# Layer 0 attention: the value product of a query tile once for all eight key/value heads, on four column groups, with the transposed probabilities in one tile per key tile

## The chip, the core and the metric

The kernel runs on one core of a Trainium2 chip. The core has five engines with an instruction stream each: TensorE (PE in the profile, with its weight loads as PEld), VectorE (DVE), ScalarE (ACT), GpSimd (POOL) and SyncE (SP), which issues most of the DMAs. Each works through its own stream in order and waits for the others through semaphores. The metric is the device time of one execution in microseconds (us), lower is better. A time of a kernel is the median of several executions; a profile is one further execution with the hardware profiler on.

## The reference, cut to what matters

Two transformer layers on 4 sequences of 256 tokens with 512 features, all in float32. Each layer is an attention and a feed-forward product, each followed by a residual sum and a layer norm without scale. The change is in the attention of layer 0, which has 32 query heads of 16 features that share 8 key/value heads in groups of 4, with a causal mask:

```python
q = (x @ Wq + bq).reshape(B, S, NUM_HEADS, HEAD_DIM).transpose(0, 2, 1, 3)
k = (x @ Wk + bk).reshape(B, S, NUM_KV_HEADS, HEAD_DIM).transpose(0, 2, 1, 3)
v = (x @ Wv + bv).reshape(B, S, NUM_KV_HEADS, HEAD_DIM).transpose(0, 2, 1, 3)
...
scores = jnp.where(causal, scores, NEG)
p = jax.nn.softmax(scores, axis=-1)
out = jnp.einsum('bhqk,bhkd->bhqd', p, v)
out = out.transpose(0, 2, 1, 3).reshape(B, S, D_MODEL)
return out @ Wo + bo
```

Layer 0 goes on with a feed-forward product whose weight is dequantised in the kernel. Layer 1 has an attention with 32 heads of 128 features and a product with a ternary weight.

## The kernel before, in words

The function `block_kernel` writes both layers as one program. The order of each engine's instructions is fixed when the program is built, by a planner that follows the order of the code and moves instructions where it expects them to be ready earlier.

**Steps of layer 0.** The attention of layer 0 is cut into 64 steps `(b, qt, h, i)`: sequence `b` (0 to 3; called a column here, a sequence's two query tiles of 128 tokens), query tile `qt` (0 or 1), half `h` of the key/value heads (heads 0 to 3 or 4 to 7), and `i`, the place of the query head in its group of four. A step so has four query heads, one for each key/value head of its half. With the causal mask query tile 0 needs key tile 0 alone, query tile 1 needs key tiles 0 and 1; a step of tile 1 is twice as wide.

**What a step does.** `begin0` (L473): two matmuls make the scores of four heads (L482, on two row groups of 32 rows), DVE adds the mask (L487) and takes the negative row maxima (L490), ACT takes four exponentials with their sums (L274). Dividing by the sums (`divided`, L278: a reciprocal on DVE at L279, a product on POOL at L282) is put off to the next step. `transpose0` (L506): TensorE transposes the four heads' probabilities, one key tile to a PSUM bank (L297), and DVE and ACT in turn copy the banks to SBUF (`evacuate`, L95; its instructions show as L100 on DVE and L102 on ACT). `end0` (L520): at the last `i` of a half, the values are multiplied with the transposed probabilities of the four places `i` together (L531).

**The value product.** A key/value head has 16 features, and two of them (even and odd, `e` = 0 and 1) share 32 output partitions: the weights `v` of one head are 128 keys x 32, with zeros in the 16 columns of the other head. Each matmul has 128 rows, 32 columns and 512 moving elements (4 places x 128 queries) and writes 32 of the 128 partitions of one PSUM bank `o`: partitions `32 * r` on, where `r = 2 * h + j` is a pair of heads. So a half `h` writes two of the four groups of 32 columns, in turn, and the other half writes the other two, four steps later. After the second half the bank is copied to `oT` and a `tail0` generator is started.

**The pipeline.** `run` (L323) does, for each n: begin step n, one piece of fill work, transpose step n - 3 (`lag=3`), end step n - 5 (`lag` and `more=2`). Fill work is the projections of the next column (`project0`: L386, L399, L414) and the tails (`tail0`: output product L438, residual sum L440, norm L257 to L264, transpose L270, feed-forward product L455, sum L459, second norm, transpose to `x2T`).

**Buffers.** The scores have two PSUM tiles of two banks each (`ps_s0`), so the scores of step n wait for the exponentials of step n - 2. Three banks (`ps_w`) go round among transposes and products. One bank is for `o` (`ps_o0`). The transposed probabilities of a half are one SBUF tile with room for two key tiles, `[P, 2, G, 4, 4, 32]`, 16 KB a partition, in two buffers.

**After layer 0.** Layer 1 begins with its projections in Strassen's form (`Quarters`, L619, products L632) beside the last tails, and then runs 64 steps of its own attention (L968 to L1027) with the output product in Strassen's form (L881).

Of the kernel before, what the change touches and what calls it, by code (L numbers as in the profile page):

```python
# [12 lines left out]
F32 = mybir.dt.float32  # L13
# [7 lines left out]
P = 128  # L21
# [3 lines left out]
NKV, G = 8, 4  # L25
BLK = 32
ROWS = 64
EPS = 1e-5
MASKED = -3.0e38

# [19 lines left out]
def distance_table():  # L52

    rel = P + np.arange(P)[:, None] - np.arange(2 * P)[None, :]
    dist = -np.sqrt(np.maximum(rel, 0).astype(np.float32))
    return np.where(rel >= 0, dist, np.float32(MASKED)).astype(np.float32)


@with_exitstack
def block_kernel(  # L60
# [23 lines left out]
    def pool(stack, name, bufs=1, **kw):  # L84
        return stack.enter_context(tc.tile_pool(name=name, bufs=bufs, **kw))
# [9 lines left out]
    def evacuate(dst, src):  # L95

        if not last:
            turn[0] ^= 1
        if turn[0] and not last:
            nc.vector.tensor_copy(dst, src)  # L100
        else:
            nc.scalar.copy(dst, src)  # L102
# [20 lines left out]
    a0 = pool(la, "a0", 2, side="right")  # L123
    causal = wa.tile([P, P], F32, name="causal")
    make_causal_mask(nc, causal, MASKED)
    ps_w = pool(ctx, "ps_w", 3, space=PSUM)
    ps_s0 = pool(la, "ps_s0", 2, space=PSUM)
    ps_o0 = pool(la, "ps_o0", 1, space=PSUM)
# [5 lines left out]
    def bank_m(name):  # L134
        return ps_w.tile([P, D], F32, tag="w", name=name)
# [116 lines left out]
    def norm_factors(y, name):  # L252

        st = s0.tile([P, 6], F32, tag="bn", name=f"bn_{name}", bufs=4)
        mv = s0.tile([P, 2], F32, tag="mv", name=f"mv_{name}", bufs=4)
        rs = s0.tile([P, 1], F32, tag="rs", name=f"rs_{name}", bufs=4)
        nc.vector.bn_stats(st, y)  # L257
        nc.vector.bn_aggr(mv, st)
        nc.vector.tensor_scalar(rs, mv[:, 1:2], EPS, 1.0, ALU.add, ALU.mult)
        powers.append(nc.gpsimd.tensor_tensor(rs, rs, minus_half, ALU.pow))  # L260
        return mv[:, 0:1], rs

    def normalise(dst, y, factors):
        nc.vector.tensor_scalar(dst, y, *factors, ALU.subtract, ALU.mult)  # L264

    def transposed(dst, src, name):

        pt = bank_t(f"pt_{name}")
        for c in range(NC):
            nc.tensor.transpose(pt[:, c, :], src[:, ts(c, P)], ident)  # L270
        evacuate(dst, pt)
# [20 lines left out]
    def transposed_probabilities(name, pr, parts):  # L292

        for kt, dst in parts:
            pt = bank_t(f"pt_{name}_{kt}")
            for i in range(G):
                nc.tensor.transpose(pt[:, i, :], pr[:, i, ts(kt, P)], ident)  # L297
            evacuate(dst, pt.rearrange("p i (j q) -> p i j q", q=32))
# [135 lines left out]
    def tail0(tt, oT):  # L434

        py = bank_m(f"py_{tt}")
        for i in range(G):
            nc.tensor.matmul(py, oT[:, i, :], wop[:, i, :], start=(i == 0), stop=(i == G - 1))  # L438
        y = s0.tile([P, D], F32, tag="y", name=f"y_{tt}")
        nc.vector.tensor_tensor(y, py, x[tt], ALU.add)  # L440
        factors = norm_factors(y, f"a{tt}")
        yield True
        x1 = s0.tile([P, D], F32, tag="x1", name=f"x1_{tt}")
        normalise(x1, y, factors)
        yield True
        if tt < NTT - 1:
            yield True
            yield True
        x1T = s0.tile([P, NC, P], F32, tag="x1T", name=f"x1T_{tt}")
        transposed(x1T, x1, f"x1_{tt}")  # L450
        nc.gpsimd.tensor_tensor(x1, x1, fb_b, ALU.add)
        yield True
        pf = bank_m(f"pf_{tt}")
        for c in range(NC):
            nc.tensor.matmul(  # L455
                pf, x1T[:, c, :], wfT[:, c, :], start=(c == 0), stop=(c == NC - 1)
            )
        y2 = s0.tile([P, D], F32, tag="y", name=f"y2_{tt}")
        nc.vector.tensor_tensor(y2, pf, x1, ALU.add)  # L459
        factors = norm_factors(y2, f"b{tt}")  # L460
        yield True
        x2[tt] = xp.tile([P, D], F32, tag="x", name=f"x2_{tt}")
        normalise(x2[tt], y2, factors)
        yield True
        if tt < NTT - 1:
            yield True
            yield True
        transposed(x2T[:, :, ts(tt, P)], x2[tt], f"x2_{tt}")
        yield True

    ahead, tails = deque(), deque()
# [25 lines left out]
    open0 = {}  # L497
# [8 lines left out]
    def transpose0(b, qt, h, i, pr):  # L506
        name = f"0_{b}_{qt}_{h}_{i}"
        if i == 0:
            open0["p", h] = a0.tile(
                [P, 2, G, 4, 4, 32], F32, tag="prT", name=f"prT0_{b}_{qt}_{h}"  # L510
            )
        prT = open0["p", h]
        transposed_probabilities(
            name,
            pr,
            [(kt, prT[:, kt, i].rearrange("p j n q -> p n j q")) for kt in range(qt + 1)],
        )
        return prT

    def end0(b, qt, h, i, prT):  # L520
        if i < G - 1:
            return
        if h == 0:
            open0["o"] = ps_o0.tile([P, G * P], F32, tag="o", name=f"o0_{b}_{qt}")
        o = open0["o"]
        v = qkv0[b][2]
        for kt in range(qt + 1):
            for e in range(2):
                for j in range(2):
                    r = 2 * h + j  # L530
                    nc.tensor.matmul(  # L531
                        o[32 * r : 32 * r + 32, :],
                        v[:, kt, r, ts(e, 32)],
                        prT[:, kt, :, :, 2 * j + e, :],
                        start=(kt == 0 and e == 0),
                        stop=(kt == qt and e == 1),
                    )
        if h == 1:
            oT = a0.tile([P, G, P], F32, tag="oT", name=f"oT0_{b}_{qt}")
            evacuate(oT.rearrange("p i q -> p (i q)"), o)  # L540
            tails.append(tail0(2 * b + qt, oT))

    def before0(step):
        b, qt, h, i = step
# [11 lines left out]
    def fill():  # L556
# [6 lines left out]
        [(b, qt, h, i) for b in range(B) for qt in range(2) for h in range(2) for i in range(G)],  # L563
        begin0,
        transpose0,
        end0,
        before0,
        fill,
# [534 lines left out]
```

## Time and profile before

| | |
|---|---|
| median of 3 executions | 973.0 us (971.88 to 973.82) |
| profiled execution, own time | 970.91 us |
| its span | 968.9 us |
| PE busy | 939.5 us, 97% |
| DVE busy | 619.7 us, 64% |
| POOL busy | 445.6 us, 46% |
| ACT busy | 316.3 us, 33% |
| DMA, mean | 77 GB/s |
| granted TensorE clock, mean | 0.995 |

The span runs from the first to the last recorded instruction; the device time has some 2 us more around it. A float32 matmul shows as two records (two passes), each with a weight load of its own. Matmul durations are modelled and reach past the start of the next matmul, so a busy share of PE includes short stalls. The attention of layer 0 ends at about 276 us of the span.

### The profile page before, as it was taken

The numbers are of one execution on the slowest core, as the hardware profiler recorded it, in microseconds if no ns is written. First come the engines' busy times: TensorE is split into PE (matmuls) and PEld (weight loads), VectorE is DVE, ScalarE is ACT, GpSimd is POOL, SyncE is SP. The second block draws the span as 40 slices with busy tenths as digits, with TensorE's granted clock in tenths as the row PEclk, the third lists the DMA queues.
The fourth block names the chain that finished last, engine by engine and source line by source line (L and its number), as shares of the span: only waits on it lengthen the run. The fifth ranks groups of instructions, "written<-read, shape, count | busy, mean of one in ns | idle before, by whom it ended". The sixth has DMA issues, their size and how long they took to land.

```text
span 968.9 us, 11389 instructions
## 1 busy us (share of the span) xinstructions
PE 939.5 (97%) x3593; PEld 556.0 (57%) x3593; DVE 619.7 (64%) x1291; ACT 316.3 (33%) x1194; POOL 445.6 (46%) x461
## 2 busy tenths in 40 slices
PE   7999999999899999999999999999999999999996
PEld 5645555554344445566666666666666666666652
DVE  3876767777633446665666665766676666666566
ACT  2664564555511002333222222122222212224441
POOL 3463552644446213444533553444633634556732
PEclk9999999999999999999999999999999999999998
DMA  9500000000020011354443443433443334332001
GB/s 237 185 1 1 1 1 1 1 1 1 1 87 0 22 44 39 103 139 120 122 134 90 123 133 109 130 109 87 131 130 91 128 77 119 113 105 69 1 33 55
DMA packets 76418, 74.45 MB, mean 77 GB/s; under 512 B 5957, under 2 KB 52678, under 8 KB 76358
## 3 DMA queue, kind: packets, MB, share of 16 engines
q1 hardware_dynamic: 75014, 72.02, 26.1%
q10 hardware_dynamic: 1344, 1.70, 0.6%
q8 instruction: 29, 0.48, 0.2%
q14 instruction: 31, 0.25, 0.1%
HBM read 49.58 MB, written 24.12 MB: 76 GB/s over the span
## 4 chain that ended last, share of the span: by engine, by line
PE 82%; POOL 9%; DVE 5%; ACT 2%; DMA 1%; issue 1%; ACTq 0%; POOLq 0%; DVEq 0%
PE p_q L632 18%; PE po L881 14%; PE sc L968 7%; PE o L1008 7%; PE p_k L632 5%; PE p_v L632 5%; PE o L531 5%; PE sc L482 4%; PE pt L297 3%; PE pq L399 3%; PE py L438 3%; PE pf L455 3%; PE py L842 2%; POOL pr L282 2%; POOL x L903 2%; ACT pr L274 1%
## 5 line engine op out<-in xcount | busy, mean ns | idle before, releaser
L274 ACT ACTIVATE pr<-sc,nm 128x256 f32<-128x256 f32 (+1 forms) x512 | 209.4, 420 | 364.7 <-DVE nm L984 277.2
L282 POOL TENSOR_TENSOR pr<-pr,sums 128x512 f32<-128x512 f32 (+1 forms) x128 | 190.1, 1485 | 232.1 <-DVE sums L279 223.9
L976 DVE SCALAR_TENSOR_TENSOR sc<-table,sc 128x128 f32<-128x128 f32 (+1 forms) x256 | 86.0, 356 | 34.7 <-PE sc L968 32.4
L274 ACT ACTIVATION_READ_ACCUMULATOR pr<-sc,nm 128x1 f32 x512 | 103.5, 202 | 0.0
L968 PEld LDWEIGHTS sc<-kT,qT 128*128 128x128 f32 x512 | 82.3, 191 | 35.1 <-issue 29.7
L968 PE MATMUL sc<-kT,qT 128*128 128x256 f32 (+1 forms) x512 | 95.0, 327 | 0.0
L1008 PE MATMUL o<-prT,v 128*128 128x512 f32 x192 | 92.8, 592 | 0.0
L308 DVE STREAM_TRANSPOSE blocks<-pr 128x512 f32<-128x512 f32 x84 | 57.6, 698 | 45.2 <-POOL pr L282 45.2
L646 DVE TENSOR_TENSOR qT<-p_q,qT 128x512 f32<-128x512 f32 x96 | 64.6, 685 | 33.6 <-PE p_q L632 32.8
L984 DVE TENSOR_REDUCE nm<-sc 128x2 f32<-128x512 f32 (+1 forms) x128 | 69.9, 550 | 1.5
L297 PE MATMUL pt<-ident,pr 128*128 128x128 f32 x432 | 62.6, 278 | 6.0 <-POOL pr L282 5.3
L297 PEld LDWEIGHTS pt<-ident,pr 128*128 128x128 f32 x432 | 49.3, 142 | 32.5 <-issue 17.1
L490 DVE TENSOR_REDUCE nm<-sc 128x4 f32<-128x512 f32 (+1 forms) x64 | 61.0, 953 | 1.1
L482 PE MATMUL sc<-kT,qT 32*128 32x256 f32 (+1 forms) x256 | 59.9, 533 | 1.6 <-ACT pr L274 1.6
L487 DVE TENSOR_TENSOR sc<-sc,causal 128x512 f32<-128x512 f32 x64 | 44.3, 692 | 26.5 <-PE sc L482 26.2
L881 PE MATMUL po<-wo,so 128*128 128x256 f32 x224 | 58.0, 381 | 2.1 <-POOL so L612 2.1
L632 PE MATMUL p_q<-x2T,ws_q 128*128 128x512 f32 x128 | 59.8, 592 | 0.0
L102 ACT COPY o<-o 128x512 f32<-128x512 f32 x29 | 17.0, 586 | 124.9 <-PE o L1008 124.9
L632 PE MATMUL p_q<-xt,ws_q 128*128 128x512 f32 x128 | 57.7, 592 | 0.0
L881 PE MATMUL po<-wo,o 128*128 128x256 f32 x224 | 57.7, 380 | 0.0
L632 PE MATMUL p_q<-x2T,wq 128*128 128x512 f32 x128 | 57.6, 592 | 0.0
L881 PE MATMUL po<-to,so 128*128 128x256 f32 x224 | 53.3, 381 | 1.0 <-POOL so L615 1.0
(155 smaller groups left out, 1435.2 us busy)
## 6 DMA issues: line engine op xcount, KB each, us to landing
way<-blocks SPq DMA_DIRECT2D x112, 128.0 KB, 2.5
prT<-way SPq DMA_DIRECT2D x28, 512.0 KB, 3.7
wq<-in_L_attn_w_qkv_dram SPq DMA_DIRECT2D x8, 1024.0 KB, 5.3
wo<-in_L_attn_w_o_dram SPq DMA_DIRECT2D x8, 1024.0 KB, 5.4
way<-blocks SPq DMA_DIRECT2D x112, 64.0 KB, 1.8
prT<-way SPq DMA_DIRECT2D x28, 256.0 KB, 2.6
wk<-in_L_attn_w_qkv_dram SPq DMA_DIRECT2D x4, 512.0 KB, 3.7
wv<-in_L_attn_w_qkv_dram SPq DMA_DIRECT2D x2, 1024.0 KB, 6.3
```

Of the source, the lines that this page charges most:

```text
L274: nc.scalar.activation(pr[:, i, 0:w], sc, AF.Exp, bias=nm[:, i : i + 1], accum_out=sums[:, i : i + 1])
L282: nc.gpsimd.tensor_tensor(pr[:, :, 0:w], pr[:, :, 0:w], sums.unsqueeze(2).to_broadcast([P, G, w]), ALU.mult)
L297: nc.tensor.transpose(pt[:, i, :], pr[:, i, ts(kt, P)], ident)
L482: nc.tensor.matmul(sc[:, j, :, 0:w], qT[rows, i, ts(qt, P)], kT[rows, :, 0:w], start=True, stop=True)
L490: nc.vector.tensor_reduce(nm, scf[:, :, 0:w], AX.X, ALU.max, negate=True)
L632: nc.tensor.matmul(bank, fixed, moving, start=(c == 0), stop=(c == 1))
L646: add = lambda dst, a, b: nc.vector.tensor_tensor(dst, a, b, ALU.add)
L881: nc.tensor.matmul(bank[:, ts(n, HALF)], left[:, c, :], right[:, c, :], start=(c == 0), stop=(c == 1),)
L968: nc.tensor.matmul(sc[:, m, 0:w], qT[:, 2 * j + m, b * S + qt * P : b * S + (qt + 1) * P], kT[:, b * S : b * S + w], start=True, stop=True,)
L976: nc.vector.scalar_tensor_tensor(sc[:, m, 0:w], table[:, 2 * P - w :], slopes[kv * G + 2 * j + m], sc[:, m, 0:w], ALU.mult, ALU.add,)
L984: nc.vector.tensor_reduce(nm[:, 2 * j : 2 * j + 2], sc[:, :, 0:w], AX.X, ALU.max, negate=True)
L1008: nc.tensor.matmul(o, v1[:, 2 * b + kt, ts(kv, P)], prT[:, kt].rearrange("p j h q -> p h j q"), start=(kt == 0), stop=(kt == qt),)
```

## The change

`end0` now returns at once except at the last step of a query tile, `(h, i) == (1, 3)`. There it does the value product of all eight key/value heads: for each key tile (now from the last to the first) and each parity, four matmuls in the order `r = 2, 3, 0, 1`, one on each group of 32 columns. The matmuls themselves, their shapes, number and the bank they write are as before. `transpose0` writes to tiles of one key tile, `[P, G, 4, 4, 32]`, 8 KB a partition, one for each half and key tile, from five buffers, and hands on the tiles of both halves.

```diff
         if i == 0:
-            open0["p", h] = a0.tile(
-                [P, 2, G, 4, 4, 32], F32, tag="prT", name=f"prT0_{b}_{qt}_{h}"
-            )
-        prT = open0["p", h]
+            open0[h] = [
+                a0.tile(
+                    [P, G, 4, 4, 32], F32, tag="prT", name=f"prT0_{b}_{qt}_{h}_{kt}", bufs=5
+                )
+                for kt in range(qt + 1)
+            ]
         transposed_probabilities(
             name,
             pr,
-            [(kt, prT[:, kt, i].rearrange("p j n q -> p n j q")) for kt in range(qt + 1)],
+            [(kt, open0[h][kt][:, i].rearrange("p j n q -> p n j q")) for kt in range(qt + 1)],
         )
-        return prT
+        return open0[0], open0[1] if h else None
 
     def end0(b, qt, h, i, prT):
-        if i < G - 1:
+        if (h, i) != (1, G - 1):
             return
-        if h == 0:
-            open0["o"] = ps_o0.tile([P, G * P], F32, tag="o", name=f"o0_{b}_{qt}")
-        o = open0["o"]
+        o = ps_o0.tile([P, G * P], F32, tag="o", name=f"o0_{b}_{qt}")
         v = qkv0[b][2]
-        for kt in range(qt + 1):
+        for kt in range(qt, -1, -1):
             for e in range(2):
-                for j in range(2):
-                    r = 2 * h + j
+                for r in (2, 3, 0, 1):
                     nc.tensor.matmul(
                         o[32 * r : 32 * r + 32, :],
                         v[:, kt, r, ts(e, 32)],
-                        prT[:, kt, :, :, 2 * j + e, :],
-                        start=(kt == 0 and e == 0),
-                        stop=(kt == qt and e == 1),
+                        prT[r // 2][kt][:, :, :, 2 * (r % 2) + e, :],
+                        start=(kt == qt and e == 0),
+                        stop=(kt == 0 and e == 1),
                     )
-        if h == 1:
-            oT = a0.tile([P, G, P], F32, tag="oT", name=f"oT0_{b}_{qt}")
-            evacuate(oT.rearrange("p i q -> p (i q)"), o)
-            tails.append(tail0(2 * b + qt, oT))
+        oT = a0.tile([P, G, P], F32, tag="oT", name=f"oT0_{b}_{qt}")
+        evacuate(oT.rearrange("p i q -> p (i q)"), o)
+        tails.append(tail0(2 * b + qt, oT))
```

## The prediction

> **What bounds the kernel now.** I read the page first: shares of the engines, then the chain of work that ended last.
>
> ```profile
> PE 939.5 (97%) x3593; PEld 556.0 (57%) x3593; DVE 619.7 (64%) x1291; ACT 316.3 (33%) x1194; POOL 445.6 (46%) x461
> PE 82%; POOL 9%; DVE 5%; ACT 2%; DMA 1%; issue 1%; ACTq 0%; POOLq 0%; DVEq 0%
> PE p_q L632 18%; PE po L881 14%; PE sc L968 7%; PE o L1008 7%; PE p_k L632 5%; PE p_v L632 5%; PE o L531 5%; PE sc L482 4%; PE pt L297 3%; PE pq L399 3%; PE py L438 3%; PE pf L455 3%; PE py L842 2%; POOL pr L282 2%; POOL x L903 2%; ACT pr L274 1%
> ```
>
> TensorE is the bound, and the value product of layer 0 (o, L531) has 5% of the span on the chain, 48 us. Groups of the first 330 us (busy us, mean ns of one record | idle before) and busy times by stretch (PE, PEld, DVE, ACT, POOL) show how nearly all of it is on the path:
>
> ```profile
> L531 PE MATMUL o<-prT,v 128*32 128x512 f32 x192 | 47.7, 607 | 0.6 <-DVE prT L100 0.6
> L438 PE MATMUL py<-wop,oT 128*128 128x512 f32 x64 | 29.6, 605 | 1.3 <-DVE oT L100 1.3
> ...
> 40.00:280.00 240.00, 232.48 (x1104) 119.14 (x1101) 167.77 (x316) 128.76 (x506) 112.38 (x86) 0.99 0.00 1
> ```
>
> 192 records are 96 matmuls of two passes. In layer 0 PE has 97%, DVE 70%, ACT 54%, POOL 47%: there is room, but the other engines are not far behind. The timeline of one burst (start, us) says how fast the passes go:
>
> ```profile
> 52.37 1.91 PE L531 MATMUL o<-prT,v 128*32 128x512 f32 x8
> 54.21 1.13 PE L482 MATMUL sc<-kT,qT 32*128 32x512 f32 x4
> ...
> 52.37 0.14 PEld L531 LDWEIGHTS o<-prT,v 128*32 128x32 f32 x4 [0.17 <-issue]
> 52.82 0.12 PEld L531 LDWEIGHTS o<-prT,v 128*32 128x32 f32 x2 [0.31 <-issue]
> 53.25 0.12 PEld L531 LDWEIGHTS o<-prT,v 128*32 128x32 f32 x2 [0.31 <-issue]
> ```
>
> Eight passes take 1.84 us to the next work; eight passes of py, the same length over all 128 columns, show as 3.70. Two weight loads, 0.11 each, fit in 0.12, and a new pair comes every 0.43. So the two column groups of a half run side by side, a pair of passes each 0.43 us, and the other two groups stand idle. Sequence by sequence the chain has two bursts of 1.84 (tile 0) and two of 3.56 (tile 1).
>
> **The Trainium skill.** "TensorE: Matmul & The Clock Gate", Part 3 (Packing small matmuls): matmuls on different column groups run concurrently, measured 2.38x with three groups and 10.6x with sixteen row-and-column tiles. The pairs above agree for two; no run here shows four. "TensorEngine Tiling (Array Packing)", Key Properties: tiles load weights and multiply independently, changing the tiling mode drains the array. The trace agrees in kind: each burst begins with a gap before its loads, 0.17 above. The first page, Part 1: after an idle window the clock falls to half. The trace shows it once, 0.96 granted in 240 to 280 us. It matters at the end.
>
> **The change, part by part.** *Removed:* the bursts of the first half, one for each query tile. 96 of the 192 passes, 48 pairs of 0.43 us = 20.6 us, with their beginnings 4 x (1.84 + 3.56) = 21.6. *Added:* the same passes join the second half's bursts. If four groups run as two do, a round of four takes 0.43 and those bursts keep 1.84 and 3.56; a stagger of some 7 ns a group is nothing. Copies into the new tiles have the same number and size. Five buffers are enough: four tiles of a tile-1 group and the first of the next group, or two and the first two of the next, never more than five, so no wait is added. Last key tile first means that the first matmul waits for the newest copy, but transposes run two steps ahead of ends, over 3 us: free; without that cover, a copy (0.6 to 0.7) at each of eight bursts, 5 us. No DMA moves and no queue but the engines' own changes.
>
> So the ceiling is 21.6, and the question is what waits next at each removed burst. The next scores need the exponentials of two steps before, so each site has its own slack.
>
> *First column, tile 0 (39.6 us).* Later scores start 2.9, 1.6, 1.5 and 0.2 us after their banks were free, and those banks move up too. I give 0.2 back: **1.65** of 1.84.
>
> *Tile 1, three times (68, 134, 201 us, alike).* PE, then ACT:
>
> ```profile
> 134.58 3.63 PE L531 MATMUL o<-prT,v 128*32 128x512 f32 x16
> 138.14 0.70 PE L482 MATMUL sc<-kT,qT 32*128 32x256 f32 x4
> 138.77 0.66 PE L270 MATMUL pt_x<-ident,x 128*128 128x128 f32 x4
> 139.26 1.04 PE L297 MATMUL pt<-ident,pr 128*128 128x128 f32 x8
> 140.23 0.70 PE L482 MATMUL sc<-kT,qT 32*128 32x256 f32 x4
> 140.86 3.70 PE L455 MATMUL pf<-wfT,x1T 128*128 128x512 f32 x8
> ...
> 135.59 0.21 ACT L274 ACTIVATION_READ_ACCUMULATOR pr<-sc,nm 128x1 f32 x1
> 137.61 0.21 ACT L274 ACTIVATION_READ_ACCUMULATOR pr<-sc,nm 128x1 f32 x1
> ```
>
> The scores at 138.14 need exponentials that end at 135.80, those at 140.23 need 137.82. In the changed order pt_x moves ahead of the first, one matmul of pf ahead of the second, and ACT copies x1T before the second's exponentials (0.6 later, 138.4). From 134.58: pt_x to 135.1; wait, scores 135.85 to 136.5; transposes to 137.35; one pf matmul to 138.2; scores 138.45 to 139.1; three pf matmuls of 0.86 to 141.7. Before, pf ended at 140.86 + 3.43 = 144.3. **2.5** each of 3.56 (worked 2.6).
>
> *Tile 0 of columns 1 and 2 (101, 168 us).*
>
> ```profile
> 101.47 1.91 PE L531 MATMUL o<-prT,v 128*32 128x512 f32 x8
> 103.31 1.13 PE L482 MATMUL sc<-kT,qT 32*128 32x512 f32 x4
> ...
> 105.39 1.13 PE L482 MATMUL sc<-kT,qT 32*128 32x512 f32 x4
> ...
> 104.77 0.21 ACT L274 ACTIVATION_READ_ACCUMULATOR pr<-sc,nm 128x1 f32 x1
> ```
>
> The scores at 105.39 need exponentials that end at 104.98, of scores older than the burst: they can't move. Again one pf matmul (0.86) goes ahead of them and fills the gap; pf ends at 108.8 for 109.9. **1.1** of 1.84.
>
> *Their second bursts.* ACT now does a step's exponentials before the copy of `oT`, and half of a later score pair stands ahead of py: py 1.1 later. But DVE then takes mask and row maxima before the norm's last operation, whose wait for POOL (0.67) and the work around it come off the chain: 1.4 earlier. **0.3** each, the least certain term.
>
> *Last column.* No projections are left. DVE runs nearly full between its two tails, and a walk through it leaves 0.7 at the py of 246.5. Behind, PE waits for POOL at 258.3, the half clock comes, and o of the first half holds PE from 261.3 to 265.6; pf starts at 266.95. Without it, pf starts at about 261.4, when its input is copied, and the last o at 267.2 for 272.07: **4.9** in all, with the clock's fall kept.
>
> Sum: 1.65 + 3 x 2.5 + 2 x 1.1 + 2 x 0.3 + 4.9 = 16.85; I take 16.5. What follows is PE work of layer 1 in an unchanged order; its value weights load when layer 0's memory comes free (issued 280.3, used at 294.6) and so move with it. Span 968.9 - 16.5 = 952.4, own time 970.9 - 16.5 = 954.4. The median of the runs is 2.1 above the profiled execution: 973.0 - 16.5 = **956.5 us**.
>
> **Rivals.** *Nothing is given back:* the ceiling, 951.4. For it: all bursts of the first half lie on the chain. Against: the exponentials' ends above.
>
> *The other engines' loop takes the place:* scores, mask, maxima, exponentials and back is 5.3 us for two steps of tile 1, and in the orders rewritten by the planner I may have missed a wait. If only the first site and the three of tile 1 pay, at 2.25 each (the slack of the first scores after them), 8.4 us: 964.6. For it: DVE's 70% and PE waits of up to 2.6 us that are already there. Against: fill work placed into two of the gaps.
>
> *Four groups do not overlap,* slower: TensorE streams two groups and the third waits. Then no pass is saved; the second bursts grow by 21.6 us, all on the chain and ahead of py, while the sites above return only 16.5: 973.0 + 5.1 = 978. For it: the trace shows pairs only, and four moving streams at once are asked of the memory. Against: the skill's sixteen tiles. It decides once a joined burst is 1.76 times as long as now (16.5 / 21.6), 3.2 us for eight pairs.
>
> **Numbers.** Forecast, 10 to 20 us gained: 0.62. Ceiling, over 20: 0.10. Loop: 0.15. No overlap: 0.11. Near zero: 0.02. A measurement here tells from no change what is over 0.2%, 2 us. Faster 0.87, same 0.02, slower 0.11. Range 952 (just above the ceiling's 951.4) to 966 (past the loop's 964.6). The overlap's bounds are 1 and 2 times the burst.
>
> **What would show it.** Right: joined bursts with 16 passes in about 1.8 and 32 in about 3.6 us; no o of a first half; busy PE of the stretch down by some 20 us; pf starts earlier by about 2.5 at each tile-1 site and scores waiting for ACT there. Wrong: joined bursts near 3.6 and 7 us, or a PE wait for a copy at their first matmul, or new half-clock stretches as PE idles more.

## The result, and the profile after

The changed kernel takes 961.6 us (median of 4 runs, 960.96 to 965.4) where the kernel before took 972.4 on the same chip (970.45 to 973.82): 10.8 us by the medians. The ratio of the means is 0.990 (95% interval 0.987 to 0.993), so about 10 us or 1.0% faster. The forecast was 956.5 us, a gain of 16.5. Some 6 us of the expected gain are missing.

The page of the changed kernel (its line numbers in this region are two higher than before; the value product is now L532) starts with the span, the shares of the engines, and, from the chain that ended last, the shares by engine and by line:

```profile
span 958.8 us, 11377 instructions
...
PE 922.0 (96%) x3593; PEld 554.1 (58%) x3593; DVE 619.4 (65%) x1291; ACT 315.2 (33%) x1194; POOL 445.6 (46%) x461
...
PE 79%; POOL 9%; DVE 6%; ACT 2%; issue 1%; DMA 1%; ACTq 0%; POOLq 0%; DVEq 0%
```

TensorE is still the bound, but its part of the chain fell from 82% to 79%. PE is busy for 17.5 us less, of which only 10.1 us are gained (968.9 - 958.8): PE waits more. The groups of the first 330 us (busy us, mean ns of one record | idle before, with its causes) say for whom. The first line is the kernel before, the others the changed kernel:

```profile
L297 PE MATMUL pt<-ident,pr 128*128 128x128 f32 x384 | 55.5, 279 | 3.6 <-POOL pr L282 3.2 <-DVE v L422 0.2
...
L299 PE MATMUL pt<-ident,pr 128*128 128x128 f32 x384 | 57.3, 285 | 9.3 <-POOL pr L284 6.2 <-ACT prT L104 2.7 <-DVE v L424 0.2
...
L532 PE MATMUL o<-prT,v 128*32 128x512 f32 x192 | 23.4, 622 | 0.7 <-ACT prT L104 0.7
```

The value product went from 47.7 to 23.4 us with the same 192 records. The transposes of the probabilities waited 3.6 us before and now wait 9.3, of which 2.7 for a copy on ScalarE, a cause that was not named there before. The stretch from 40 to 270 us (PE, PEld, DVE, ACT, POOL busy; then the granted clock), before and after:

```profile
40.00:270.00 230.00, 223.85 (x1071) 115.73 (x1068) 164.41 (x309) 128.18 (x505) 111.83 (x85) 0.99 0.00 1
...
40.00:270.00 230.00, 214.34 (x1105) 116.90 (x1102) 167.08 (x316) 127.44 (x506) 112.40 (x86) 0.98 0.00 1
```

PE is busy for 9.5 us less of the same stretch, the other engines are within 2% of before, and the clock fell from 0.99 to 0.98.

**The joined bursts.** The timeline of PE, at one of query tile 0 and one of tile 1:

```profile
50.59 1.92 PE L532 MATMUL o<-prT,v 128*32 128x512 f32 x16
52.44 1.13 PE L484 MATMUL sc<-kT,qT 32*128 32x512 f32 x4
...
80.51 3.64 PE L532 MATMUL o<-prT,v 128*32 128x512 f32 x32
84.08 0.70 PE L484 MATMUL sc<-kT,qT 32*128 32x256 f32 x4
```

Sixteen passes take 1.85 us to the next work and thirty-two take 3.57, as long as eight and sixteen took before. In the records the four groups start within 20 ns (0, 6, 13, 20), the next four 0.45 us later and the rest every 0.43. The four groups overlap fully.

**The place of a removed burst of tile 1**, the first of three alike:

```profile
64.70 0.70 PE L484 MATMUL sc<-kT,qT 32*128 32x256 f32 x4 [0.34 <-ACT pr L276]
65.33 1.09 PE L299 MATMUL pt<-ident,pr 128*128 128x128 f32 x8
66.27 0.63 PE L272 MATMUL pt_x<-ident,x 128*128 128x128 f32 x4
67.61 0.70 PE L484 MATMUL sc<-kT,qT 32*128 32x256 f32 x4 [0.71 <-ACT pr L276]
```

Where the burst was, the transpose of `x1` (pt_x) moved in, and the scores wait 0.71 us for the exponentials. That is the forecast picture.

**The joined burst of tile 0 in the second column** is where the first loss lies. PE in the kernel before and in the changed one, then ScalarE in the changed one:

```profile
117.28 1.16 PE L297 MATMUL pt<-ident,pr 128*128 128x128 f32 x8
118.38 1.91 PE L531 MATMUL o<-prT,v 128*32 128x512 f32 x8
120.22 1.13 PE L482 MATMUL sc<-kT,qT 32*128 32x512 f32 x4
121.27 3.70 PE L438 MATMUL py<-wop,oT 128*128 128x512 f32 x8
```

```profile
112.01 0.63 PE L299 MATMUL pt<-ident,pr 128*128 128x128 f32 x4
113.99 1.12 PE L299 MATMUL pt<-ident,pr 128*128 128x128 f32 x4 [1.35 <-ACT prT L104]
115.04 3.08 PE L532 MATMUL o<-prT,v 128*32 128x512 f32 x16
118.05 1.98 PE L484 MATMUL sc<-kT,qT 32*128 32x512 f32 x6
119.96 3.70 PE L440 MATMUL py<-wop,oT 128*128 128x512 f32 x8
```

```profile
111.53 0.47 ACT L276 ACTIVATE pr<-sc,nm 128x256 f32<-128x256 f32 x1 [5.37 <-DVE sums L281]
...
113.34 1.08 ACT L104 COPY prT<-pt 128x512 f32<-128x512 f32 x2
```

The second four transposes wait 1.35 us for a bank that ScalarE has to empty, and ScalarE does so only after four exponentials, for which it sat waiting on VectorE until 111.53. Then the burst takes 3.0 us instead of 1.85, since one stretch of 3.4 us from 114.0 runs at half clock. And six records of scores, not four, stand ahead of `py`: half of a later pair has been drawn ahead. Before, the eight transposes went through in one piece.

**Where the gain came and went.** The start of each piece of PE's work, counted from the first scores of the profile and compared with the same start in the kernel before, gives the gain by stretch (us). The columns "changed" and "repetition" are two profiles of the changed kernel. The other two are experiments described below: swapped copies with idle products, and these with the key tiles in rising order.

| stretch | forecast | changed | repetition | swap + idle products | swap + idle products, rising order |
|---|---|---|---|---|---|
| first column, tile 0 | 1.65 | 1.61 | 1.61 | 1.61 | 1.60 |
| tile-1 sites (3) | 2.5, 2.5, 2.5 | 2.74, 3.28, 3.28 | 2.74, 3.29, 3.27 | 2.74, 2.73, 2.72 | 2.43, 2.43, 2.43 |
| tile 0 of columns 1, 2 | 1.1, 1.1 | 0.86, 0.86 | 0.86, 0.86 | 0.86, 0.86 | 0.67, 0.66 |
| their second bursts | 0.3, 0.3 | -3.96, -2.34 | -2.34, -2.34 | -0.89, -0.89 | -0.01, -0.01 |
| last column | 4.9 | 3.95 | 0.53 | 6.12 | 5.51 |
| all else | 0 | -0.37 | -0.30 | -1.20 | -0.21 |
| sum | 16.85 | 9.91 | 8.18 | 14.66 | 15.50 |

"All else" includes the end of the kernel, where every profile falls to half clock for 6.8 to 10.6 us; 0.9 of the 1.20 in the fourth column of numbers is lost there. At the end of layer 0 the last two columns are level, 15.5 each.

### The profile page after: what moved, and what is told of

Its sections match the earlier page's. It is cut to its first block, busy times and chain, and to the rows that moved or that the text cites. A ratio compares the mean times of both kernels' runs of the same rounds, so it can differ in the third digit from the quotient of the medians.

```text
span 958.8 us, 11377 instructions
## 1 busy us (share of the span) xinstructions
PE 922.0 (96%) x3593; PEld 554.1 (58%) x3593; DVE 619.4 (65%) x1291; ACT 315.2 (33%) x1194; POOL 445.6 (46%) x461
## 4 chain that ended last, share of the span: by engine, by line
PE 79%; POOL 9%; DVE 6%; ACT 2%; issue 1%; DMA 1%; ACTq 0%; POOLq 0%; DVEq 0%
PE p_q L632 18%; PE po L881 14%; PE sc L968 7%; PE o L1008 7%; PE p_k L632 5%; PE p_v L632 5%; PE sc L484 4%; PE pt L299 3%; PE py L440 3%; PE pf L457 3%; PE o L532 2%; PE pq L401 2%; POOL pr L284 2%; ACT pr L276 2%; PE py L842 2%; POOL x L903 2%
```

## The experiments

The times are medians, and each ratio is against runs of the kernel before on the same chip. The theory after the first profiles: the overlap gives what was forecast, and the gain is lost to (a) a bank wait behind ScalarE at the second bursts of columns 1 and 2, which the split tiles bring, lengthened by a late VectorE, and (b) stretches in which TensorE, which waits more than before, is granted half its clock. The rival to (a) is that the removed bursts had merely hidden a slower loop of the other engines.

**x_tiles_only: the split tiles alone, two bursts for each query tile as before**

```diff
-            open0["p", h] = a0.tile([P, 2, G, 4, 4, 32], F32, tag="prT", ...)
+            open0["p", h] = [
+                a0.tile([P, G, 4, 4, 32], F32, tag="prT", ..., bufs=5)
+                for kt in range(qt + 1)
+            ]
...
```

> The kernel before with the second part of the change alone: transposed probabilities in tiles of one key tile from five buffers, value products still by halves on two column groups. By the prediction it costs nothing (within 1 us of before). Theory 'copy behind the exponentials': the split changes which bank the second transposes of the step (1, 0, 1) get, so PE waits there for ACT in columns 1 and 2, some 1.3 us each: 1 to 3 us slower than before.

976.3 us (7 runs), ratio 1.0045 (1.0029 to 1.0062): 4.4 us slower than before. PE waits at the place of (a) without any joined burst:

```profile
117.77 0.63 PE L297 MATMUL pt<-ident,pr 128*128 128x128 f32 x4
119.74 0.66 PE L297 MATMUL pt<-ident,pr 128*128 128x128 f32 x4 [1.34 <-ACT prT L102]
```

So the edit for which the prediction added no wait costs 4.4 us alone: in the profile 1.46 us at each of the two sites, and at the second 1.6 more with a half-clock stretch that begins there. The joined product is worth 1.5% (1.0045 less 0.9898), 14.3 us, beside it. Around this wait the streams hold the same instructions in the same order on TensorE, VectorE and ScalarE as before; what differs is the bank. In the program before, the second transposes of step (1, 0, 1) get the bank that VectorE had emptied last; with the split tiles, in these two columns, they get the one that ScalarE empties. Why the planner hands out the banks differently isn't known. The counterpart, a joined product from the old tiles, wasn't run: it needs a third buffer of 16 KB, for which the kernel has no room.

**x_swap: at one step of columns 1 and 2 the copies change engines**

```diff
+        swap = (qt, h, i) == (1, 0, 0) and b in (1, 2)
+        turn[0] ^= swap
         transposed_probabilities(...)
+        turn[0] ^= swap
```

> The changed kernel with one difference: at the step (qt, h, i) = (1, 0, 0) of columns 1 and 2 the two copies of the transposed probabilities change engines, so the first bank is emptied by DVE and the second by ACT. Theory 'copy behind the exponentials': in the changed kernel PE stood 1.35 us before the second transposes of the next step, because the bank it gets is emptied by ACT behind four exponentials that wait for DVE; that wait and with it the later start of the joined burst (10.1 us after the tail's sum instead of 8.1 before) should shrink by 1.5 to 2 us in each of two columns, 3 to 4 us in all: about 957.5 to 958.5 where the changed kernel has 961.4. Rival 'the DVE chain is the bound anyway': the wait only moves to the next scores, which need the same exponentials, and under 1 us comes of it.

960.6 us (6 runs, 957.1 to 966.42), ratio 0.9889 (0.9865 to 0.9913). The wait is gone, with all eight transposes in one piece:

```profile
113.97 1.16 PE L299 MATMUL pt<-ident,pr 128*128 128x128 f32 x8
115.06 1.92 PE L535 MATMUL o<-prT,v 128*32 128x512 f32 x16
```

At the fourth column's start this profile is 3.45 us ahead of the changed kernel's first one. Of that 1.6 are the half-clock stretch of that profile at 114.0; against the repetition, which has none there, it is 1.84. So theory (a) holds for the wait, and the 3 to 4 us expected were too many. The last column then runs at half clock for 13.7 us from 219.6 and 6.8 us from 257.1 and returns it all; the median is within the noise of the changed kernel's. The time of this kernel follows the clock: the execution granted 0.995 took 957.1 us, the one granted 0.986 took 966.4.

**x_late_add and x_swap_add: POOL's residual sums moved behind the value projection, without and with the swap**

```diff
-            if i > 1:
-                tt = 2 * b + i - 2
-                tc.keep_in_program_order(nc.gpsimd.tensor_tensor(x[tt], x[tt], bo_b, ALU.add))
...
+        for tt in range(2 * b, 2 * b + 2):
+            tc.keep_in_program_order(nc.gpsimd.tensor_tensor(x[tt], x[tt], bo_b, ALU.add))
```

> The changed kernel with the sums x + bo of a column (POOL, 1.26 us each, two a column) moved from after the third and fourth query projection to after the value projection. Theory: in the changed kernel the norm's last operation on DVE takes 1.48 us instead of 0.55 in columns 1 and 2 because such a sum runs on POOL beside it, and it is now on the chain (after pf, before the exponentials that the joined burst waits for): 0.9 us a column, 1.8 us in all. Rival: the chain has other slack there, under 0.5 us; or the sums meet another step on POOL and cost 1 us.

> Both of the above together. If both waits lie one behind the other on the same chain they add: 4.5 to 5.5 us faster than the changed kernel, about 956 to 957. If PE becomes the bound again after the first, less than the sum.

963.1 us (0.9907, 0.9887 to 0.9927) and 965.1 us (0.9922, 0.9905 to 0.9939). The normalisation on VectorE that makes ScalarE late had met the sum on POOL, and doesn't any more; groups of the changed kernel and of x_late_add:

```profile
L266 DVE TENSOR_SCALAR x<-y,mv_b,rs_b 128x512 f32<-128x512 f32 x8 | 6.2, 774 | 1.9 <-POOL rs_b L262 1.9
```

```profile
L266 DVE TENSOR_SCALAR x<-y,mv_b,rs_b 128x512 f32<-128x512 f32 x8 | 4.3, 540 | 1.9 <-POOL rs_b L262 1.9
```

In x_late_add, what the bank wait costs at the second burst of column 2 fell from 1.49 to 0.55 us, by about the 0.93 that the collision had cost, so the link is real; but 0.9 us were lost at each of two places in the first column, and both kernels ran 13.6 us of the last column at half clock. Neither came near its expectation, and beyond the clock and those two places it isn't explained.

**x_pairs: the joined product, one pair of groups after the other**

```diff
-        for kt in range(qt, -1, -1):
-            for e in range(2):
-                for r in (2, 3, 0, 1):
+        for pair in ((2, 3), (0, 1)):
+            for kt in range(qt, -1, -1):
+                for e in range(2):
+                    for r in pair:
...
```

> Joint product as in the changed kernel, but the column groups work in two pairs, one pair after the other, so that at most two groups overlap. Theory (the gain is the four-group overlap): the bursts take 3.5 and 7.0 us instead of 1.8 and 3.5, 4 x 5.25 = 21 us more of TensorE in the first stage, nearly all on its path, so 975 to 983 us: nothing of the gain is left, since the split tiles alone cost 4.4 us. Rival (the gain comes from there being one site of products for each query tile instead of two, with the accumulator's wait and its copy): at least half of the gain stays, 962 to 968 us.

972.3 us (14 runs), ratio 1.0009 (0.9996 to 1.0023): the gain is gone, though not as far as 975. The experiment did only half of what it was for. The program's stream has all passes of the first pair ahead of the second pair's, but TensorE did not keep to two groups:

```profile
81.16 5.38 PE L533 MATMUL o<-prT,v 128*32 128x512 f32 x32
```

The burst takes 5.3 us to the next work, neither 3.6 nor 7. In the records its passes start two by two for four rounds, then four by four for four rounds, then two by two again: the second pair starts while the first has half of its passes to go. In the 16-pass bursts all four groups start within 33 ns, and the time stays 1.87 us. So only the four tile-1 bursts lost half of their overlap, 1.75 us each, and at the first three the profile falls behind by 1.75, 3.49 and 5.21 us against the changed kernel's repetition: nothing of it is hidden. The fourth (1.75) and 6.8 us more of half clock in the last column (some 3.4) make up the rest of the 10 us.

**x_plain_order: key tiles rising, groups 0 to 3**

```diff
-        for kt in range(qt, -1, -1):
+        for kt in range(qt + 1):
             for e in range(2):
-                for r in (2, 3, 0, 1):
+                for r in range(4):
```

> The changed kernel with the key tiles in rising order and the column groups as 0, 1, 2, 3, instead of the last key tile first and the groups of the second head pair first. The prediction called the order free. Theory: the four groups overlap in any order, so the bursts stay at 1.8 and 3.5 us and the time within 1.5 us of the changed kernel: 960 to 963 us. Rival: the order matters because the newest copies of transposed probabilities come last, and each of the eight bursts waits up to half a us for one: 964 to 966 us, with a wait for a copy shown ahead of the bursts.

961.4 us (0.9899, 0.9886 to 0.9912), as expected: four groups overlap in either order, and the products themselves wait for a copy only once, 0.6 us, as in the kernel before. What the order changes is the planner's arrangement: 0.85 us of the loss at each of the two second bursts is gone (no half score pair ahead of `py`), while the tile-1 sites give 0.3 less.

**x_swap_warm: idle products in the last column's waits, with the swapped copies.** Seven products that nothing reads stand ahead of transposes that wait there (the lines of the swap are left out):

```diff
+        warm = {(0, 1): 2, (0, 2): 1, (1, 1): 3, (1, 2): 1}.get((qt, i), 0) if b == 3 and h else 0
+        if warm:
+            spare = ps_o0.tile([P, G * P], F32, tag="o", name=f"o_{name}")
+            for _ in range(warm):
+                w = G * P if i == 1 else 2 * P
+                nc.tensor.matmul(spare[:, 0:w], ident, wfT[:, 0, 0:w], start=True, stop=True)
         transposed_probabilities(...)
```

> The swapped copies of x_swap, and in the last column seven idle products (identity times the feed-forward weight, 128 rows, into the free accumulator bank, never read) ahead of the transposes that wait there for probabilities: 5.1 us of TensorE work in waits that were 1.6, 0.4, 2.6 and 0.5 us long. They compute nothing that is used. Theory (the half-clock windows follow windows in which TensorE streams too little, and they are what the swap lost): no half-clock window after 205 us of the span, granted clock 0.995 or more, 956 to 958.5 us and less spread between runs than x_swap had (957.1 to 966.4). Rival (the half clock comes whatever TensorE does there): half-clock windows stay at about 220 and 257 us, and the products add up to 3 us: 961 to 964 us.

956.3 us (4 runs, 955.16 to 958.47), ratio 0.9852 (0.9837 to 0.9866). Windows of x_swap and of this kernel (columns as above):

```profile
216.00:234.00 18.00, 15.99 (x46) 6.86 (x45) 9.22 (x20) 8.50 (x35) 6.99 (x6) 0.62 0.00 1
250.00:262.00 12.00, 8.65 (x41) 5.57 (x40) 7.49 (x13) 6.47 (x21) 7.12 (x5) 0.80 0.00 1
```

```profile
216.00:234.00 18.00, 16.88 (x83) 7.45 (x83) 15.15 (x27) 11.99 (x51) 10.27 (x8) 1.00 0.01 1
250.00:262.00 12.00, 10.51 (x59) 4.65 (x57) 4.15 (x8) 1.17 (x2) 2.91 (x3) 1.00 0.00 0
```

In 18 us the first gets through 46 records of PE at 0.62 of the clock and the second through 83 at full clock, six of them idle products. (The second's work lies 2.8 us earlier in its span; over the matching 18 us it is 81.) Work that computes nothing made the kernel about 4 us faster (3.6 by the ratios, whose intervals just touch), and its runs were granted 0.996 to 0.997 where x_swap's had 0.986 to 0.995. Theory (b) holds: the waits are the same waits, filled, and no profile with such products has a stretch at half clock in layer 0.

**x_warm: the idle products without the swap. x_before_warm: the kernel before with three of them in its longest wait**

> The changed kernel with the seven idle products of x_swap_warm in the last column, and without the swapped copies. Theory (two causes that add: the waits for the bank behind ScalarE cost 1.5 us at each of two sites, the half clock of the last column the rest): x_swap_warm's 956.3 plus 3 to 4, so 959 to 960.5 us, no half-clock window after 205 us of the span; one may remain near 114 us. Rival (the idle products alone bring it, the bank waits are covered): 956 to 957.5 us.

> The kernel before with three idle products (2.55 us of TensorE) in its longest wait of the last column, 2.59 us at 255.7 us of the span. Theory: its profile has one half-clock window of 3.4 us at 259.6, with a busy TensorE, so at most 1.7 us are to be had: 969 to 970 us beside 971.0. So most of the 14 us between it and x_swap_warm is the joint product, the smaller part the clock. Rival (idle products bring the kernel before as much as they brought x_swap, 4 us and more): 967 us or less.

959.0 us (0.9874, 0.9857 to 0.9891) and 968.6 us (0.9973, 0.9964 to 0.9981), with no stretch at half clock in their layer 0. The first lies 2.7 us above x_swap_warm (2.1 by the ratios, with intervals that overlap; 1.8 in layer 0 of the profiles), which is the bank wait, and 2.9 below the changed kernel's repetition (961.9; 3.0 by the ratios), which is the clock. The second gains 3.0 us on its kernel before (971.6), more than the 1 to 2 expected and less than the rival's 4: its last column is 2.7 us ahead, of which 1.7 at most are the half-clock stretch (half of its 3.4 us, an estimate). The idle products also moved one product behind the transposes that it had stood between, which may be the rest. Between the two warmed kernels lie 9.5 us: the change is worth about 10 us with or without the clock's falls in layer 0, so the measured gain isn't an effect of them.

**x_swap_warm_plain: all three**

> x_swap_warm with the key tiles in rising order and the column groups as 0, 1, 2, 3. In the profile of x_plain_order the 0.85 us that the changed kernel loses after each joined product of the first query tile in the second and third column (half a score pair put ahead of the output projection) was absent, and 0.3 to 0.5 us were lost at the second query tile of the first two columns. Theory: both carry over, net 0.5 to 1.3 us faster than x_swap_warm: 955 to 955.8 us. Rival: the planner's order changes again with the swapped copies, and the two are equal within 0.5 us.

955.3 us (4 runs, 954.74 to 957.66), ratio 0.9846 (0.983 to 0.9862), 16.3 us below the kernel before of these runs (971.6). The last column of the table shows both losses at the second bursts gone. It is 1.0 us below x_swap_warm (0.6 by the ratios), with overlapping intervals, and layer 0 of the two profiles gains the same 15.5 us, since the other sites give back what the second bursts win. So this last step is not shown to gain anything; both beat the kernel before and the changed one.

**x_after_again: the changed kernel once more**

> The changed kernel unaltered, as the measure for the other three on this chip. 961.6 us within 1 us if the first measurement stands; in the profile the same losses of 3.1 and 1.5 us ahead of the products of the second and third column's first query tile, since they come from the order of the copies; half-clock windows may lie elsewhere.

961.9 us (6 runs), ratio 0.9905 (0.9889 to 0.9922). The second bursts lose 2.34 us in both columns; the 3.96 of the first profile was this and half of a 3.4 us stretch at half clock. In the last column this profile has 13.6 us at half clock and the first 6.8, and they gain 0.53 and 3.95 us there: the difference, 3.42 us, is half of the 6.8 us between them.

## Why the prediction was right, and where it was not

- *Four groups overlap, the bursts keep 1.84 and 3.56 us:* right to 0.02 us, and with it the size of what was removed. The Trainium skill ("TensorE: Matmul & The Clock Gate", Part 3) pointed the right way; it lists three column groups at 2.38 times, and four gave the full factor of two over two groups here. The rival of no overlap is out.
- *The site terms of the first burst in each query tile:* 1.65 measured 1.61; 2.5 measured 2.74 (3.28 in columns 1 and 2 of the changed kernel, where some of the 2.34 us lost just before comes back; 2.73 there with the swap); 1.1 measured 0.86. Their mechanism, scores that wait for ScalarE's exponentials with fill work drawn into the gap, is what the timeline shows.
- *"Their second bursts", 0.3 each, is the step that failed.* They lost 2.34 us each. Of it 1.49 is the bank wait, gone with the swap (2.34 to 0.89), and 0.85 the half score pair ahead of `py`, gone with the plain order. The prediction saw the second, as 1.1, and set 1.4 us for VectorE's order against it; no profile shows such a gain, not even those where the bank wait is gone (-0.89 and -0.01).
- *The split tiles, "so no wait is added":* wrong, and this is what brought the bank wait. Buffers were counted and banks weren't. Alone the split costs 4.4 us.
- *Last key tile first is free:* right in time (961.4 and 961.9), though by two effects that cancel.
- *Last column, 4.9 "with the clock's fall kept":* the fall wasn't kept but grew. 3.95 and 0.53 in two profiles, 6.12 with idle products. The kernel before would gain 2.7 of these too without its own fall, so like for like the term is about 3.4, and 4.9 was too much by 1.5.
- *"New half-clock stretches as PE idles more"* stood among the signs of being wrong, but with no price in the sum. They cost 1.6 us in the second column (3.96 less 2.34) and 2.2 in the last (6.12 less 3.95) in the first profile, and 5.6 in the last column of the repetition (6.12 less 0.53; x_warm, without the swap, gains 6.13 there).
- *The rival of the other engines' loop*, 964.6, came nearer to 961.6 than the forecast did, but by another road: it had the missed wait right, and not that only the first site and the three of tile 1 pay. Tile 0 of columns 1 and 2 pays 0.86 each in every profile of that order, and the last column 6.1 where the clock holds.

With bank wait and clock mended, the sum comes to 15.5 us of the forecast's 16.85. That is against a kernel before that keeps its own half-clock stretch; without that it is 12.8 by the profiles (15.5 less 2.7), and 13.3 by the medians of x_before_warm and x_swap_warm_plain.

## What to carry to other kernels

When products move to idle column groups, price the sum of what each site's next wait leaves, and then follow the banks: a copy on an engine that works in order is as late as everything queued before it, and a tile split can change which copy that is. When a change makes the bounding TensorE wait more, look whether its clock still holds in the stretches that stream least. Filling a wait with products that nobody reads is worth a try there: it gained about 3 to 4 us in each of three kernels here.

## What the runs showed of the hardware

- **Partial waits are enough to halve the clock.** The Trainium skill ("TensorE: Matmul & The Clock Gate", Part 1) puts the fall after an idle window of some 3.4 us. Here no window had to be idle. In each of the thirteen profiles the stretches at half clock begin whole multiples of 3.41 us apart. The sixteen falls in layer 0 came after windows of that length in which TensorE had streamed 25 to 44% of the time (worked out from the records, with 0.43 us for 512 moving elements); none came after a busier window, and nine windows of 38 to 44% on the same grid, two in layer 0 and seven in layer 1, were not followed by one. The one fall in layer 0 of the kernel before, which the prediction put down to an idle window, followed one of 26%. The longest wait of TensorE in layer 0 of the changed kernel was 2.60 us. There a stretch at half clock lasted 3.4 to 13.7 us in the profiles.
- **A column group overtakes.** In x_pairs the passes of the second pair, later in the stream, started 26 ns after those of the first pair in short bursts, and with half of the first pair's passes still to start in long ones. The order of the program doesn't keep groups apart.
- **VectorE beside GpSimd.** The normalisation of 128 x 512 took 1.48 us when GpSimd began a sum of the same size just before it and 0.55 us without. The Trainium skill ("SBUF — State Buffer", Who interferes with whom) has this (one of the two blocks for the whole of the other's instruction), and the trace agrees in kind. In the changed kernel 1.19 of the 1.48 us lie inside the sum, and the normalisation ended 0.29 us after it:

```profile
107.40 1.26 POOL L409 TENSOR_TENSOR x<-x,bo_b 128x512 f32<-128x512 f32 x1
107.47 1.48 DVE L266 TENSOR_SCALAR x<-y,mv_b,rs_b 128x512 f32<-128x512 f32 x1 [0.27 <-POOL rs_b L262]
```

It was so in the kernel before too (777 ns in the mean of the same eight operations), behind a busy TensorE.
